# Four sparse graph layers on one core: own rows fetched before the variance's power, two PSUM buffers for the plain sums, nine places for own rows

## The chip, the cores and the metric

The kernel runs on one core of a Trainium2 chip. Its time is the device time of one execution in microseconds (us); the figure compared is the median over runs.

## The reference

Four graph layers follow each other on `x` (2708 × 512, float32) with one adjacency matrix `adj` (2708 × 2708), of which about 0.15% is not zero, besides the diagonal. Each layer is followed by a residual sum and a layer norm. The change acts on layer 1, and on buffers of layers 0 and 3.

```python
def _L1_gnn_ref(x, adj_a, adj_b, W_sa, a_sa, W_gcnb, b_gcnb, Wa, ba, Wb, bb):   # adj_a is adj_b here
    type_sum_a = adj_a @ x
    attn_a = sigmoid(concat([type_sum_a, x], 1) @ Wa.T + ba)      # attn_b: same with Wb, bb
    h = x @ W_sa
    scores = (h @ a_sa[0, :Hd])[:, None] + (h @ a_sa[0, Hd:])[None, :]
    e = where(adj_a != 0, exp(-leaky_relu(scores, 0.01)), 0.0)
    attn = e / (sum(e, 1, keepdims=True) + 1e-05)
    x_a = attn @ h
    x_b = adj_b @ (x @ W_gcnb) + b_gcnb
    return sigmoid(attn_a * x_a + attn_b * x_b)

x = layernorm(x + L0(x, adj, ...))     # L0: (x - (adj @ x) * (diag + 1)) @ W + b
x = layernorm(x + L1(x, adj, adj, ...))
x = layernorm(x + L2(x, adj))
x = layernorm(x + L3(x, adj, ...))
```

## The kernel before

The work is cut into 24 blocks of 113 rows of the graph. Layer 0 finds the non-zero entries of each block's rows (up to 512 in a block) and keeps them as a list; from then on a layer does not read `adj` any more. It fetches the rows that a block's list names, in four chunks of 128 (`gather`, four indirect DMAs issued by POOL, line 600), spreads the list into a small matrix of 128 × 113 per chunk, and lets PE multiply the two. The order of all instructions is written out by hand, engine by engine in program order; the tile framework adds the waits.

Layer 0 also writes, window by window of 128 rows, a table in DRAM (`table[0]`) with the two products `x @ W_sa` and `x @ W_gcnb` side by side and a few columns more, 1029 floats a row (`W1`). Layer 1 runs over the blocks in one loop (line 1629). Pass i, in program order:

- `gather1(i + 2)`: the fetch of the rows for block i + 2 (POOL), into one of three buffers `gath`.
- `sums1(i)`, line 1427: the plain sums of block i on PE, in a PSUM tile `l1s` of two banks. Its pool `ps_1s` has one buffer.
- `both1(i - 1)`, lines 1472 to 1487 (VectorE, called DVE; then a tanh on ScalarE, called ACT): takes the scored sums of block i − 1 out of PSUM, together with the block's own row of the table (`own1[i - 1]`). That is the last use of that own row.
- `values1`: spreads a list into a matrix, on ACT.
- `scored_sums1(i)`, line 1437: the sums weighted with `e`, on PE, in a PSUM tile `l1e` with one buffer (`ps_1e`).
- `scores1(i + 1)`, line 1410 on: the scores of the next block on DVE. It reads the fetched rows of block i + 1.
- `stats1(i - 1)`, lines 1492 to 1510: mean and variance on DVE. In every even pass the reciprocal root of two blocks' variances is computed as a power on POOL (line 1509).
- `gather_own1(i - 1 + NO)`, line 1382: one indirect DMA by POOL, which fetches a later block's own rows into the place that `both1(i - 1)` has freed. `NO` is 6, the number of places.
- `gates1(i)`, `gated1(i)`, lines 1447 to 1466: take the plain sums out of PSUM (DVE and ACT); line 1457 (`l1b`) reads the own row and is the last reader of the plain sums.
- `mask1(i + 1)`, `scale1`, `norm1(i - 2)`: the mask of the next block's scores, a factor from the power, and the finished rows of block i − 2, stored to `table[1]` by SP.

Each engine works through its own part of this list in order. The first six own rows are loaded by SP at the end of layer 0 (`load_own1`, two DMAs each). The six places lie in memory that layer 0 used for other things:

```python
    NO = 6

    def own_place(i):
        return (*shared, w0_own)[i % NO // 2][:, i % 2 * W1 :][:, :W1]
```

The buffers `xi` (two, the block's `x` rows), `uT` (two, a window turned for PE; also in layer 3) and `uw` (three, a window's inputs turned) of layer 0 come from a pool.

Of the kernel before, what the change touches and what calls it, by code (L numbers as in the profile page):

```python
# [8 lines left out]
FP = mybir.dt.float32  # L9
# [3 lines left out]
P = 128  # L13
# [434 lines left out]
def sparse_stack(  # L448
# [30 lines left out]
    N, D = x.shape  # L479
# [3 lines left out]
    NB = (N + R - 1) // R  # L483
    DB = D // P
# [79 lines left out]
    def move_rows(r, dst, src):  # L564

        c = r // 16 * 16
        for a, b in ((0, c), (c, r)):
            if a < b:
                nc.sync.dma_start(out=dst(a, b), in_=src(a, b))

    def turned(u, r, name):

        tr = ps_tr.tile([P, DB, P], FP, tag="tr", name=f"tr_{name}")
        for f in range(DB):
            nc.tensor.transpose(tr[:, f, :r], u[:r, f * P : (f + 1) * P], ident[:r, :r])
        uT = work.tile([P, DB, P], FP, tag="uT", name=f"uT_{name}")
        nc.scalar.copy(uT[:, :, :r], tr[:, :, :r])  # L577
        return uT

# [46 lines left out]

    w0_own = big.tile([P, 2 * W1], FP, name="w0_sb")
    w0_sb = w0_own[:, : DB * D].rearrange("p (b d) -> p b d", d=D)
    NO = 6

    def own_place(i):
        return (*shared, w0_own)[i % NO // 2][:, i % 2 * W1 :][:, :W1]

    def load_own1(i):
        r = rows(i)
        own1[i] = own_place(i)
        move_rows(
            r, lambda a, b: own1[i][a:b, 1 : 2 * D + 1],
            lambda a, b: table[0][i * R + a : i * R + b, 1 : 2 * D + 1],
        )  # L640
# [7 lines left out]
    with ExitStack() as phase:  # L648
# [40 lines left out]

        def load_own(i):  # L690
            r = rows(i)
            xi = work.tile([P, D], FP, tag="xi", name=f"xi{i}")
            move_rows(r, lambda a, b: xi[a:b, :], lambda a, b: x[i * R + a : i * R + b, :])
            return xi

# [122 lines left out]
        def turn_w(k):  # L818
            ps = ps_tr.tile([P, DB, P], FP, tag="tr", name=f"w_sa_t{k}")
            for f in range(DB):  # L820
                nc.tensor.transpose(ps[:, f, :], w_sa_sb[:, f, k * P : (k + 1) * P], ident)
            wT = work.tile([P, DB, P], FP, tag="uT", name=f"w_saT{k}")
            nc.scalar.copy(wT, ps)
            w_saT[k] = wT

# [225 lines left out]
        def store0(w):  # L1051
            r = wrows(w)
            st, o = st0.pop(w)
            nc.scalar.copy(st[:r, D + 1 : 2 * D + 1], o[:r, :])
            move_rows(
                r, lambda a, b: table[0][w * P + a : w * P + b, :], lambda a, b: st[a:b, :]
            )
# [3 lines left out]
        def turn_u(i):  # L1061

            u, r = u0.pop(i), rows(i)
            tr = ps_tr.tile([P, DB, P], FP, tag="tr", name=f"tr_l0_{i}")
            for f in range(DB):
                nc.tensor.transpose(tr[:, f, :r], u[:r, f * P : (f + 1) * P], ident[:r, :r])
            a = i * R
            while a < i * R + r:
                w = a // P
                b = min(i * R + r, (w + 1) * P)  # L1070
                if w not in window_uT:
                    window_uT[w] = work.tile(
                        [P, DB, P], FP, tag="uw", name=f"uw{w}", bufs=3
                    )
                nc.scalar.copy(
                    window_uT[w][:, :, a - w * P : b - w * P], tr[:, :, a - i * R : b - i * R]
                )
                a = b
# [130 lines left out]
        for k in range(NB + 2):  # L1209
            m = k + 2  # L1210
            w, wx, rest = window_at.get(k), window_at.get(k - 1), window_at.get(k - 1)
            bare = 2 < k < NB and w is None
            after = 2 < k < NB and wx is None
            parts = 4
            if any(t not in window_at for t in (k + 1, k + 2, k + 3)) and 2 < k < NB - 4:
                parts = 5
            if bare:
                parts, rest = 2, None
            if after:
                parts, rest = 3, window_at[k - 2]  # L1220
            if wx is not None and k <= NB:
                turn_x(wx)
            if m < NB:
                ranges(m)
                mark(m)
                fetch(m)
            if w is not None:
                project0(w)
            if k == 1:
                times_a(2)  # L1230
                times_a(3)
            if k == 0:
                times_a(0)
                turn_w(2)
            if unstored:
                store0(unstored.pop())
            if k + 3 < NB:
                negatives(k + 3)
            search(1)
            if m < NB:  # L1240
                pick(m)
                own[m] = load_own(m)
                values0(m)
            if k == 1:
                score_rows()
            if w is not None:
                bias0(w)
            search(1)
            if w is not None:
                residual0(w)  # L1250
            if window_at.get(k + 1, 0) > 1:
                load_window(window_at[k + 1])
            search(parts - 2)
            if wx is not None and not bare:
                next0(wx)
            if w is not None:
                norm0(w)
            if k + 1 < NB:
                sums0(k + 1)
                inputs0(k + 1)  # L1260
            if k == 1:
                score_columns()
            if k + 2 == NB:
                worst = check_lists()
                for i in range(4):
                    load_own1(i)
            if k == 0:
                times_a(1)
                turn_w(3)
            if bare:  # L1270
                starts(m + 1)
                next0(wx)
            elif rest is not None:
                rest0(rest, lambda: turn_x(w) if k == NB else starts(m + 1) if m + 1 < NB else None)
                unstored.append(rest)
            elif m + 1 < NB:
                starts(m + 1)
            if k + 1 < NB:
                turn_u(k + 1)
            if k == NB:  # L1280
                tell(worst)
                for i in range(4, NO):
                    load_own1(i)
        keep_busy(4)
        store0(KB - 1)


    gpool = ctx.enter_context(tc.tile_pool(name="gpool", bufs=1))
# [65 lines left out]
    nc.vector.memset(root, -0.5)  # L1354
    edge_s, edge_e, sum_s, sum_e, vb1, gate1, v1, mv2, unscaled = ({} for _ in range(9))
    phase = ctx.enter_context(ExitStack())
    ps_1s = phase.enter_context(tc.tile_pool(name="ps_1s", bufs=1, space=bass.MemoryType.PSUM))
    ps_1e = phase.enter_context(tc.tile_pool(name="ps_1e", bufs=1, space=bass.MemoryType.PSUM))
    ps_sp = phase.enter_context(tc.tile_pool(name="ps_sp", bufs=2, space=bass.MemoryType.PSUM))

# [19 lines left out]
    def gather_own1(i):  # L1380
        own1[i] = own_place(i)
        nc.gpsimd.indirect_dma_start(
            out=own1[i],
            out_offset=None,
            in_=table[0][:, :],
            in_offset=bass.IndirectOffsetOnAxis(ap=own_at[:, i : i + 1], axis=0),
            bounds_check=last,
            oob_is_err=False,
        )
# [17 lines left out]
    def scores1(i):  # L1407

        e = spool.tile([P, EC, R], FP, tag="e", name=f"e{i}")
        nc.vector.tensor_tensor(  # L1410
            e, gath[i % NGB][:, :, SR : SR + 1].to_broadcast([P, EC, R]),
            over_chunks(s_left[:, i, :]), ALU.add,
        )
        nc.vector.scalar_tensor_tensor(e, e, 0.01, e, op0=ALU.mult, op1=ALU.max)
        nc.scalar.activation(e, e, AF.Exp, scale=-1.0)
        edge_e[i] = e
# [212 lines left out]
    for i in range(NB):  # L1629
        if i + 2 < NB:  # L1630
            gather1(i + 2)
        sums1(i)
        if i > 0:
            both1(i - 1)
        if i + 2 < NB:
            values1(i + 2, (0, 1))
        scored_sums1(i)
        if i + 1 == NB:
            turn_norm(0)
            turn_norm(1)  # L1640
        if i + 1 < NB:
            scores1(i + 1)
        if 0 < i < NB - 1:
            stats1(i - 1)
        if 0 < i and i - 1 + NO < NB:
            gather_own1(i - 1 + NO)
        gates1(i)
        if i + 2 < NB:
            values1(i + 2, (2, 3))
        gated1(i)  # L1650
        if i + 1 < NB:
            mask1(i + 1)
        else:
            stats1(i - 1)
        scale1()
        if i > 1:
            norm1(i - 2)
        if i + 1 == NB:
            norm1(i - 1)
        if i + 1 == NB:  # L1660
            nc.sync.dma_start(out=b3_bc[0:1, :], in_=b3[None, :])
            nc.sync.dma_start(out=w3_sb, in_=w3T.rearrange("(b p) o -> p b o", p=P))
        if i < KB:
            source_sum(i)
        if i == KB:
            source_sums_out()
            row_norms(slice(0, KB))
# [243 lines left out]
```

## Time and profile before

| | us |
|---|---|
| median of 3 runs (lowest, highest) | 967.66 (964.5, 969.7) |
| the profiled execution: its own time | 978.13 |
| the profiled execution: span from first to last instruction | 976.3 |
| layer 0, until the first fetch of layer 1 | 413.9 |
| layer 1's passes, first plain sum to last scored sum | 421.9 to 614.7 |
| first sum of layer 2; of layer 3 | 630.0; 782.6 |

| engine | busy us | share of the span |
|---|---|---|
| PE matmul | 890.9 | 91% |
| DVE | 685.3 | 70% |
| ACT | 525.3 | 54% |
| POOL | 466.5 | 48% |

The profile comes from one execution. Times in it are microseconds from the first instruction. A row names the start, the duration, the engine, the line of the kernel, the operation, and what is written from what is read; a number in brackets behind it is how long the engine stood idle just before, and what ended that. "issue" there means that the profile shows nothing that the engine waited for. PE is the matmul engine, PEld its weight loads, SP issues plain DMAs. The shares above are averages over stages with different limits.

### The profile page before, as it was taken

To read this page: it belongs to the slowest core of one execution; us is meant where nothing else is said; L and a number is where in the kernel's file an instruction comes from. 1 tells how busy PE (TensorE), PEld (TensorE's weight loads), DVE (VectorE), ACT (ScalarE), POOL (GpSimd) and SP (SyncE) were. 2 spreads that over 40 slices of the span, in tenths; PEclk is the share of its full clock that TensorE was granted. 3 is DMA by queue.
4 is the path that set the end of the run, shared out by engine and by line. 5 is a ranking of instruction groups with operands and counts; after the bars stand their busy time and mean duration, and the time that the engine had idled before them with its cause. 6 is when DMAs were issued, how large, how long until landed. Compare 5 with 4: busy or idle time off the path is not lost.

```text
span 976.3 us, 11098 instructions
## 1 busy us (share of the span) xinstructions
PE 890.9 (91%) x2957; PEld 495.5 (51%) x2957; DVE 685.3 (70%) x1811; ACT 525.3 (54%) x1221; POOL 466.5 (48%) x521
## 2 busy tenths in 40 slices
PE   6789999999999999998989899787878799999993
PEld 2445556555555655466767677323333334444441
DVE  7787899878898843168988888756766526555553
ACT  5686667867668743357777776333445313222221
POOL 3223232423133320067777664476767278776730
PEclk7789999999999999979999999897999889999997
DMA  9987786978887534388898985466767266555531
GB/s 243 314 205 198 213 238 188 280 215 225 221 232 223 152 116 147 105 294 300 311 337 310 333 310 179 130 195 184 220 193 220 88 176 180 166 166 170 150 106 32
DMA packets 133758, 201.72 MB, mean 207 GB/s; under 512 B 82700, under 2 KB 82746, under 8 KB 133689
## 3 DMA queue, kind: packets, MB, share of 16 engines
q0 software_dynamic: 39456, 120.08, 39.7%
q1 hardware_dynamic: 94233, 80.86, 28.9%
q8 instruction: 25, 0.41, 0.2%
q14 instruction: 44, 0.36, 0.1%
HBM read 183.00 MB, written 27.80 MB: 216 GB/s over the span
## 4 chain that ended last, share of the span: by engine, by line
PE 62%; DVE 12%; DMA 8%; issue 6%; ACT 3%; POOL 3%; SPq 2%; another core or an unknown queue 2%; DVEq 0%; POOLq 0%; ACTq 0%
PE o_l L584 15%; PE l3a L613 9%; PE hb L584 7%; PE h L584 7%; PE l0a L613 6%; PE l2a L613 6%; DMA gath<-table,source 5%; POOL gath L600 2%; PE l1s L1427 2%; PE fetched L915 2%; PE unread L1571 2%; SPq L677 1%; PE l1e L1437 1%; DMA gath<-in_x_dram 1%
## 5 line engine op out<-in xcount | busy, mean ns | idle before, releaser
L600 POOL DMA_INDIRECT gath<-table,source x288 | 305.4, 1061 | 117.8 <-issue 86.1
L600 POOL DMA_INDIRECT gath<-in_x_dram,source x96 | 97.2, 1013 | 224.9 <-issue 192.1
L1427 PE MATMUL l1s<-gath,s 128*113 128x256 f32 (+3 forms) x384 | 93.9, 399 | 16.0 <-DVE l1b L1457 13.2
L613 PE MATMUL l2a<-gath,s_left 128*113 128x512 f32 (+1 forms) x192 | 95.2, 635 | 4.8 <-DMA gath<-table,source 3.6
L613 PE MATMUL l3a<-gath,s 128*113 128x512 f32 (+1 forms) x192 | 89.5, 610 | 2.8 <-DMA gath<-table,source 2.8
L1427 PEld LDWEIGHTS l1s<-gath,s 128*113 128x113 f32 (+1 forms) x384 | 68.8, 184 | 41.7 <-DVE l1b L1457 18.9
L613 PE MATMUL l0a<-gath,s 128*113 128x512 f32 (+1 forms) x192 | 87.3, 597 | 0.0
L584 PE MATMUL o_l<-shared,uT_l 128*113 128x512 f32 (+1 forms) x192 | 86.4, 592 | 0.7 <-ACT uT_l L577 0.7
L1437 PE MATMUL l1e<-gath,e 128*113 128x257 f32 (+3 forms) x384 | 87.0, 379 | 0.0
L584 PE MATMUL hb<-w_gc_sb,uT_x 128*128 128x512 f32 (+1 forms) x176 | 83.3, 601 | 0.0
L584 PE MATMUL o_l<-w_sb,uw 128*128 128x512 f32 (+1 forms) x176 | 82.5, 613 | 0.2
L584 PE MATMUL h<-w_sa_sb,uT_x 128*128 128x259 f32 (+1 forms) x352 | 80.8, 382 | 0.0
L1437 PEld LDWEIGHTS l1e<-gath,e 128*113 128x113 f32 (+1 forms) x384 | 68.1, 177 | 15.2
L584 PEld LDWEIGHTS h<-w_sa_sb,uT_x 128*128 128x128 f32 (+1 forms) x352 | 64.8, 185 | 19.8 <-issue 6.1
L1571 PE MATMUL unread<-bg_bc,ident 128*128 128x512 f32 x80 | 43.0, 652 | 23.9 <-remote 19.6
L1830 ACT ACTIVATE y<-l3v,mv_l 113x512 f32<-113x512 f32 (+1 forms) x24 | 19.5, 813 | 82.7 <-DVE mv_l L1826 72.6
L613 PEld LDWEIGHTS l2a<-gath,s_left 128*113 128x113 f32 (+1 forms) x192 | 34.1, 191 | 56.7 <-issue 40.0
L584 PEld LDWEIGHTS o_l<-shared,uT_l 128*113 128x113 f32 (+1 forms) x192 | 34.0, 178 | 48.7 <-issue 47.5
L1804 DVE SCALAR_TENSOR_TENSOR l3v<-o_l,d_inv,b_bc 113x512 f32<-113x512 f32 (+1 forms) x25 | 18.1, 729 | 51.5 <-PE o_l L584 50.7
L613 PEld LDWEIGHTS l3a<-gath,s 128*113 128x113 f32 (+1 forms) x192 | 33.0, 182 | 41.7 <-issue 39.7
L613 PEld LDWEIGHTS l0a<-gath,s 128*113 128x113 f32 (+1 forms) x192 | 33.8, 179 | 40.0 <-issue 36.3
L862 DVE FIND_INDEX8 where_all<-rec_all,shared 128x8 uint32<-128x678 f32 (+1 forms) x64 | 51.2, 800 | 0.0
(250 smaller groups left out, 1593.6 us busy)
## 6 DMA issues: line engine op xcount, KB each, us to landing
shared<-in_adj_dram SPq DMA_DIRECT2D x14, 1186.5 KB
table<-st SPq DMA_DIRECT2D x21, 514.5 KB
gath<-in_adj_dram SPq DMA_DIRECT2D x7, 1186.5 KB
gath<-in_x_dram SPq DMA_DIRECT2D x21, 256.0 KB
xi<-in_x_dram SPq DMA_DIRECT2D x23, 224.0 KB
table<-xr SPq DMA_DIRECT2D x23, 224.0 KB
table<-y SPq DMA_DIRECT2D x23, 224.0 KB
out_dram<-y SPq DMA_DIRECT2D x23, 224.0 KB
```

Of the source, the lines that this page charges most:

```text
L584: nc.tensor.matmul(o, lhsT=uT[:, f, :r], rhs=w[:, f, :], start=(f == 0), stop=(f == DB - 1))
L600: nc.gpsimd.indirect_dma_start(out=g[:, c, :n], out_offset=None, in_=src[:, :], in_offset=bass.IndirectOffsetOnAxis(ap=source[:, i, c : c ...
L613: nc.tensor.matmul(agg[:r, :], lhsT=s[:, c, :r], rhs=g[:, c, off : off + D], start=(c == 0), stop=(c == EC - 1),)
L677: nc.sync.dma_start(out=a[:TAIL, NF, :r], in_=adjT[NF * P :, at])
L862: nc.vector.max_index(out=where_all[:, i, g * 8 : (g + 1) * 8], in_max=top, in_values=seg)
L915: nc.tensor.matmul(t["fetched"][:, c, : 3 * NS], lhsT=t["q"][:, c * P : (c + 1) * P], rhs=rec_all[:, i].rearrange("p k s -> p (k s)"), sta ...
L1427: nc.tensor.matmul(sum_s[i][:r, k, : at.stop - at.start], lhsT=s[:, c, :r], rhs=g[:, c, at], start=(c == 0), stop=(c == EC - 1),)
L1437: nc.tensor.matmul(sum_e[i][:r, k, k : k + at.stop - at.start], lhsT=e[:, c, :r], rhs=g[:, c, at], start=(c == 0), stop=(c == EC - 1),)
L1571: nc.tensor.matmul(o[:, :cols], lhsT=ident, rhs=bg_bc[:, :cols], start=True, stop=True)
L1804: nc.vector.scalar_tensor_tensor(v[:r, at], o[:r, at], d_inv[:r, i : i + 1], b3_bc[:r, at], op0=ALU.mult, op1=ALU.add,)
L1830: nc.scalar.activation(y[:r, :], v[:r, :], AF.Identity, bias=mv[:r, 3:4], scale=mv[:r, 2:3])
```

## The change

Three things are edited, and the memory for one of them is found by a fourth.

- In each pass of layer 1 the fetch of an own row is issued before `stats1`, thus on POOL before the power, where it stood behind it.
- The pool of the plain sums gets two buffers in place of one: four PSUM banks where it had two.
- `NO` goes from 6 to 9. Rows 4 to 6 are loaded where 4 and 5 were, and rows 7 and 8 after the last store of layer 0; the fetches in the loop then begin with row 9.
- The places 6 to 8 lie in two new tiles, `uw_own` and `xi_own`. These hold, as slices, what were pool tiles before: `uw` (three), `xi` (two) and `uT` (two), used in the same turn as before.

```diff
+    def next_uT():
+        uT_ring.append(uT_ring.pop(0))
+        return uT_ring[-1]
...
-        uT = work.tile([P, DB, P], FP, tag="uT", name=f"uT_{name}")
+        uT = next_uT()
...
-    NO = 6
+
+    uw_own = big.tile([P, 3 * D], FP, name="uw_own")
+    uw_ring = [uw_own[:, k * D : (k + 1) * D].rearrange("p (b i) -> p b i", i=P) for k in range(3)]
+    xi_own = big.tile([P, max(4 * D, 2 * W1)], FP, name="xi_own")
+    xi_ring = [xi_own[:, k * D : (k + 1) * D] for k in range(2)]
+    uT_ring = [
+        xi_own[:, k * D : (k + 1) * D].rearrange("p (b i) -> p b i", i=P) for k in range(2, 4)
+    ]
+    NO = 9
 
     def own_place(i):
-        return (*shared, w0_own)[i % NO // 2][:, i % 2 * W1 :][:, :W1]
+        k = i % NO
+        t = (*shared, w0_own, uw_own, xi_own)[(k + (k >= 7)) // 2]
+        return t[:, (k + (k >= 7)) % 2 * W1 :][:, :W1]
...
-            xi = work.tile([P, D], FP, tag="xi", name=f"xi{i}")
+            xi = xi_ring[i % 2]
...
-            wT = work.tile([P, DB, P], FP, tag="uT", name=f"w_saT{k}")
+            wT = next_uT()
...
-                    window_uT[w] = work.tile(
-                        [P, DB, P], FP, tag="uw", name=f"uw{w}", bufs=3
-                    )
+                    window_uT[w] = uw_ring[w % 3]
...
             if k == NB:
                 tell(worst)
-                for i in range(4, NO):
+                for i in range(4, 7):
                     load_own1(i)
         keep_busy(4)
         store0(KB - 1)
+        for i in range(7, NO):
+            load_own1(i)
...
-    ps_1s = phase.enter_context(tc.tile_pool(name="ps_1s", bufs=1, space=bass.MemoryType.PSUM))
+    ps_1s = phase.enter_context(tc.tile_pool(name="ps_1s", bufs=2, space=bass.MemoryType.PSUM))
...
         if i + 1 < NB:
             scores1(i + 1)
+        if 0 < i and i - 1 + NO < NB:
+            gather_own1(i - 1 + NO)
         if 0 < i < NB - 1:
             stats1(i - 1)
-        if 0 < i and i - 1 + NO < NB:
-            gather_own1(i - 1 + NO)
         gates1(i)
```

## The prediction

> **What bounds the kernel now.** The change acts in layer 1, where a loop runs 24 passes, 0 to 23, one for each block of 113 rows. I read three views, in this order: busy time by stretch, to see who is nearly full; VectorE's (DVE's) rows in order of time, to see where that engine stops; the chain of waits, to see why. The first is the stretch from the start of pass 1 to that of pass 22; its columns are PE, PEld, DVE, ACT and POOL busy, PE clock, DMA share, GB/s.
>
> ```profile
> 433.87:601.28 167.41, 152.54 (x674) 118.58 (x673) 147.06 (x378) 123.49 (x315) 116.97 (x111) 0.99 0.89 312
> ```
>
> These are 21 passes in 167.41 us, 7.97 each. PE looks fullest, but its own work is 3.45 us of plain sums and 3.46 of scored sums per block, 6.9 in all (blocks 20 to 21, 585.40 to 592.34, where it never stops: 6.94). What does not show as busy on DVE is mostly short gaps between dependent operations. I therefore take its pace from starts. Each pass begins on DVE with the `rec` row of `both1`:
>
> ```profile
> 488.75 0.15 DVE L1472 SCALAR_TENSOR_TENSOR rec<-l1e,ediag 113x1 f32<-113x1 f32 x1
> ...
> 491.61 0.63 DVE L1410 TENSOR_TENSOR e<-gath,s_left 128x452 f32<-128x452 f32 x1 [0.77 <-issue]
> ...
> 497.40 0.15 DVE L1472 SCALAR_TENSOR_TENSOR rec<-l1e,ediag 113x1 f32<-113x1 f32 x1
> ...
> 504.86 0.15 DVE L1472 SCALAR_TENSOR_TENSOR rec<-l1e,ediag 113x1 f32<-113x1 f32 x1
> ```
>
> An odd pass (497.40 to 504.86) takes 7.46 us, and every odd pass takes 7.45 to 7.47: DVE goes straight through. An even pass, which also prepares the variance and its power, takes 7.80 where DVE does not wait (441.34 to 449.14) and more where the `e` row of `scores1` waits for gathered rows. Passes 2 to 20 last 7.80, 9.07, 8.16, 8.65, 8.33, 8.84, 8.51, 8.46, 9.28, 8.29. With 7.80 as floor the excess is 0, 1.27, 0.36, 0.85, 0.53, 1.04, 0.71, 0.66, 1.48, 0.49: **7.4 us**. Check: 11 × 7.46 + 10 × 7.80 = 160.06, and 167.41 − 160.06 = 7.35. So DVE sets the pace, and 7.4 us is all that better timing can bring in this stretch.
>
> Why the rows come late is in the chain:
>
> ```profile
> 510.60 0.46 POOL mv_l L1509
> ...
> 512.87 0.26 POOL gath L600
> ...
> 516.96 6.08 DMA gath<-table,source
> ```
>
> and on POOL's rows between these (shown here one pair of passes earlier):
>
> ```profile
> 492.01 1.10 POOL L600 DMA_INDIRECT gath<-table,source  x1 [0.30 <-issue]
> 494.74 0.71 POOL L1509 TENSOR_TENSOR mv_l<-mv_l,root 113x2 f32<-113x2 f32 x1 [1.63 <-DVE gate L1447]
> 495.63 1.07 POOL L1382 DMA_INDIRECT shared<-table,own_at  x1 [0.19 <-issue]
> 497.00 0.99 POOL L600 DMA_INDIRECT gath<-table,source  x1 [0.30 <-issue]
> ```
>
> POOL waits 1.63 us for the power's input, does the power (L1509), then issues the own rows (L1382), and only then the next block's four gathers. The last of those lands 6.08 us after its issue, just too late for the `e` two passes on. Power to power this loop takes 526.90 − 510.60 = 16.30 us; DVE alone needs 7.46 + 7.80 = 15.26. The POOL loop is longer, and closes through DVE's wait.
>
> **What the Trainium skill says.** "Perfetto Trace Analysis", Optimization Strategy: a gap that repeats on the engine that should be saturated can mean too few buffers. Here a gap repeats on PE, which is not that engine:
>
> ```profile
> PE l1s L1427 <- DVE l1b L1457: 13.2, 13, 2.0
> POOL mv_l L1509 <- DVE gate L1447: 23.9, 11, 9.2
> ```
>
> So I give the buffer no time of its own. "PSUM — Partial Sum Buffer", PSUM bank collisions raise a hardware error: two engines must not touch a bank at once, two readers included. The trace agrees: L1457 (DVE) waits 0.32 us in nearly every block for the copy L1451 (ACT) of the same sums. A second buffer leaves this pair in one bank, so 0.32 stays inside the floors. "DMA: Bandwidth & Descriptors", Issuing engines are not separate DMA queues: transfers from SP and POOL share 16 engines and only issue time is saved. In the trace the share is about 1.0 from 485 to 496 us, at a mean of 379 GB/s.
>
> **The change, part by part.**
>
> *Own rows ahead of the power (even passes).* Both instructions stay. The fetch needs its place free, that is `both1`'s L1478 done: 489.24 + 0.73 = 489.97, while POOL is idle from 493.11. So it goes out at 493.4, inside the 1.63 us wait, and ends at 494.5, before the power's input at 494.7. The gathers behind the power come 497.00 − 495.64 = 1.36 us earlier. The POOL loop falls from 16.30 to 14.94, under DVE's 15.26. Hence nearly all of the 7.4 goes. Should POOL be late, the power queues behind the fetch and up to 1.4 us passes to `scale1` on DVE; that reads it at 497.03, 1.58 after the power's end, so this is covered. What can be late next: with 0.32 us of slack, a landing slower than 6.08 (I see 5.9 to 6.5) brings back up to 0.1 to 0.4 in some passes. I take 0.6 us left over ten passes; bounds 0 and 5.4, the latter if landings follow the DMA's backlog and not the issue (below).
>
> *Two PSUM buffers.* L1427 no longer waits for L1457 (13.2 us). Scored sums keep one buffer, so PE next waits at L1437 for `both1`'s L1478. Per odd pass: L1478 ends 1.19 us after `rec`, scored sums then run 3.5, plain sums 3.4, so PE is back after some 8.2 us, 0.7 into the next pass, and waits about 0.5. It gains nothing, but scored sums end about 0.6 earlier and free the gathered rows; POOL waited 5.3 us in four places for that, in early passes and at 584.38. A loss is excluded: PE's order is the same, it only starts earlier, and the three pools take 4 + 2 + 2 banks, which the layer has to itself. I take 0; the other bound is a gain of 0.5, pass 20's excess, already in the 7.4.
>
> *Nine places.* POOL loses three fetches, those of passes 16 to 18: 3 × 1.36 = 4.1 us of POOL time, off the path, since DVE holds it; it makes pass 18 (the 1.48) safer. SP gains three loads of two issues each, about 0.3 us an issue. Row block 6: 0.6 us on SP at 404, before the store of window 20 and the moves at 407.19, which wait for ACT anyway. Its 113 × 4096 B = 0.46 MB take 1.2 us at 379 GB/s; the DMA share falls to 0.24 at 408 to 410, so it fits there. If not, `ediag` at 410.13 comes up to 1.2 later, and ACT takes its result only at 412.07, after a table load; ediag's two last DVE operations end at 410.76, so 1.3 us cover it. Rows 7 and 8: four issues, 1.2 to 1.5 us from 411.47, where SP stands waiting until 413.08 for the last store; behind them is only `bg_bc`, which PE needs at 419.92. Their 0.93 MB need 2.4 us. The DMA share is 0.10, 0.01, 0.00 from 412 to 415 and gathered data flow from 415, so they fit, just. Block 1's `e` (429.12) waits 2.01 for gathers already, so what overlaps is paid in full. I take +0.3; bounds 0 and 2.4.
>
> *Slices in place of pool tiles* (`uw`, `xi`, `uT`): same number of slots, same order of use, no instruction added. I take 0; below.
>
> Sum: −7.4 + 0.6 + 0.3 = −6.5 us. The profiled execution took 978.13 (span 976.3) and would take 971.6. It stands 10.5 above the median of 967.66; nothing says that the waits differ there, so I carry the 6.5 over: **961.2**. About 0.5% (4.8 us) is what a measurement of this kernel can tell from no change.
>
> **Rivals.**
>
> *Landings follow the backlog (0.20).* For it: the share averages 0.89 and reads 1.0 for 11 us of each pair of passes. By share the stretch has 0.89 × 167.4 = 149 us of DMA, against 160.06 of DVE. Against it: the share falls to 0.58 and 0.68 at 496 to 498, right behind POOL's stop, so an earlier issue finds idle engines. If it holds, only the excess of passes 18 and 20 (2.0 us), where fetches fall away, is won: 965.7.
>
> *The start pays (0.10).* The two late loads meet the first gathers and cost their whole 2.4 us, with the rest as forecast: about 963.6.
>
> *Slower: slices wait like whole tiles (0.08).* If an access to `xi_own` waited for all others to that tile, turning a window (`uT`, ACT) would wait for the `x` rows in flight to the same tile. Layer 0 is a PE chain with turn, `h` and `hb` in it, 22 windows; one landing per window, some 1.6 us (moves issued until 408.5 land at 410.1), is 35 us: 996. From 0.5 us a window it eats the gain and ends slower. Against it: `gath` and `shared` already hold slices with different uses in layer 0, without such waits. That the buffer does not do what it says (PE's wait moves to L1437) is in my forecast, at no price.
>
> **How the numbers follow.** My case has 0.62 and lies between 957 (all 7.4, and some 3 for the spread of the runs, 964.5 to 969.7) and 962.8. The next two end within 0.5%, 0.30 together; the fourth slower, 0.08. Range: 957 to 968, the top being the backlog's 965.7 and the runs' spread; it leaves out the fourth and the tails.
>
> **What would show it.** Right: in layer 1 L1382's counterpart stands before the power in every even pass; `e` waits for gathers fall from some 6.5 us in passes 2 to 20 to under 1.5; even passes last 7.8 to 7.9, odd ones still 7.46; PE's waits on `l1b` are gone, with waits on `l1a` in their place. Wrong: even passes over 8.2 with POOL ahead (backlog); block 1's `e` later than 429.6 counted from the first gather at 413.93 (start); layer 0 longer than now, when the first gather starts at 413.93 (slices); odd passes off 7.46, either way, would overturn the bound itself.

## The result and the profile after

The kernel with the change takes **958.98 us** (median of 11 runs, 954.93 to 963.22); the kernel before, run on the same chip in turn with it, takes 967.53 (11 runs, 963.59 to 970.87). The ratio is **0.9921, 95% interval 0.9898 to 0.9944**: a gain of 7.6 us, between 5.4 and 9.9. (The ratio is worked out over all runs and not from the two medians, which lie 8.6 us apart.) The profiled execution took 958.69, with a span of 956.9. The kernel is faster, by 0.8%; the forecast was 961.2.

The first view is again the busy time from the start of pass 1 to that of pass 22, of the kernel after. Columns: the stretch and its length, PE, PEld, DVE, ACT and POOL busy, PE clock, DMA share, GB/s.

```profile
433.71:593.84 160.13, 150.72 (x674) 117.45 (x673) 146.35 (x380) 123.17 (x315) 113.08 (x107) 1.00 0.90 316
```

The length is what counts: 160.13 us where it was 167.41. DVE's floor, worked out ahead as 11 × 7.46 + 10 × 7.80, was 160.06. So the stretch stands 0.07 us above the floor. Below, I call "excess" what the even passes 2 to 20 last beyond 7.80 each: it was 7.4 us, now it is −0.03.

VectorE's rows, after, an even pass (502.14 to 509.94) and an odd one (509.94 to 517.39):

```profile
502.14 0.15 DVE L1486 SCALAR_TENSOR_TENSOR rec<-l1e,ediag 113x1 f32<-113x1 f32 x1
...
504.13 0.62 DVE L1424 TENSOR_TENSOR e<-gath,s_left 128x452 f32<-128x452 f32 x1
...
509.94 0.15 DVE L1486 SCALAR_TENSOR_TENSOR rec<-l1e,ediag 113x1 f32<-113x1 f32 x1
...
517.39 0.15 DVE L1486 SCALAR_TENSOR_TENSOR rec<-l1e,ediag 113x1 f32<-113x1 f32 x1
```

The `e` row has no bracket any more: DVE comes to it without having waited, here and in all passes from 1 on. The even pass lasts 7.80, the odd one 7.45. GpSimd's rows between them, after:

```profile
503.80 1.28 POOL L604 DMA_INDIRECT gath<-table,source  x1 [0.30 <-issue]
505.38 1.51 POOL L1396 DMA_INDIRECT shared<-table,own_at  x1 [0.30 <-issue]
507.35 0.72 POOL L1523 TENSOR_TENSOR mv_l<-mv_l,root 113x2 f32<-113x2 f32 x1 [0.46 <-DVE gate L1461]
508.25 1.06 POOL L604 DMA_INDIRECT gath<-table,source  x1 [0.19 <-issue]
```

The own rows' fetch (L1396) now fills the time in which POOL waited for the power's input; what is left of that wait is 0.46 us, and the next gather follows the end of the power 0.19 later. From the start of the power to that of this gather it is 0.90 us, where it was 2.28 (means of nine pairs of passes). And the waits from 410 to 610 us, after (who, for whom: us in all, times, longest):

```profile
PE l1e L1451 <- DVE l1a L1492: 10.4, 23, 0.7
...
DVE l1b L1471 <- ACT row_cnt L1465: 8.5, 24, 0.8
...
DVE e L1424 <- DMA gath<-table,source: 4.0, 2, 2.5
```

PE's wait for `l1b` (13.2 us before) is gone; in its place PE waits at L1451 for `l1a`, 10.4 us. DVE's wait for gathers is left in two places only, both ahead of pass 1.

**Where the gain is.** Layer 1 as a whole, from its first gather to layer 2's first sum, fell from 216.1 us (413.9 to 630.0) to 208.0 (414.26 to 622.3): 8.1, of which 7.3 lie in the stretch above. The two profiled spans differ by 19.4, but most of the rest is layer 2, which the change doesn't touch: it took 152.6 us in the first profile of before, 142.0 after, and 143.7 in a second profile of before (`e5_before_again`).

### The profile page after: what moved, and what is told of

Same layout as the page of the kernel before. It is cut to its first block, busy times and chain, and to the rows that moved or that the text cites. A ratio compares the mean times of both kernels' runs of the same rounds, so it can differ in the third digit from the quotient of the medians.

```text
span 956.9 us, 11163 instructions
## 1 busy us (share of the span) xinstructions
PE 884.8 (92%) x2957; PEld 489.4 (51%) x2957; DVE 685.3 (72%) x1811; ACT 526.3 (55%) x1221; POOL 465.5 (49%) x518
## 4 chain that ended last, share of the span: by engine, by line
PE 58%; DMA 14%; DVE 14%; issue 5%; ACT 4%; SPq 3%; POOL 2%; POOLq 0%; DVEq 0%; ACTq 0%
PE o_l L588 15%; DMA gath<-table,source 11%; PE l3a L617 8%; PE hb L588 7%; PE h L588 7%; PE l0a L617 6%; PE l2a L617 2%; PE fetched L929 2%; POOL gath L604 2%; PE unread L1585 2%; DVE l1b L1471 1%; SPq L691 1%; DMA gath<-in_x_dram 1%; DVE l1b L1475 1%; DVE l1a L1492 1%
## 5 line engine op out<-in xcount | busy, mean ns | idle before, releaser
L617 PE MATMUL l2a<-gath,s_left 128*113 128x512 f32 (+1 forms) x192 | 97.2, 624 | 17.6 <-DMA gath<-table,source 17.4
L1451 PE MATMUL l1e<-gath,e 128*113 128x257 f32 (+3 forms) x384 | 88.4, 383 | 10.4 <-DVE l1a L1492 10.4
L1441 PE MATMUL l1s<-gath,s 128*113 128x256 f32 (+3 forms) x384 | 89.8, 387 | 0.0
L588 PE MATMUL o_l<-shared,xi_own 128*113 128x512 f32 (+1 forms) x192 | 86.5, 593 | 0.8 <-ACT xi_own L581 0.7
L588 PE MATMUL hb<-w_gc_sb,xi_own 128*128 128x512 f32 (+1 forms) x176 | 83.3, 601 | 0.0
L1451 PEld LDWEIGHTS l1e<-gath,e 128*113 128x113 f32 (+1 forms) x384 | 66.2, 177 | 32.7 <-PE l1s L1441 19.4
L588 PE MATMUL o_l<-w_sb,uw_own 128*128 128x512 f32 (+1 forms) x176 | 82.7, 614 | 0.2
L588 PE MATMUL h<-w_sa_sb,xi_own 128*128 128x259 f32 (+1 forms) x352 | 80.8, 382 | 0.0
L588 PEld LDWEIGHTS h<-w_sa_sb,xi_own 128*128 128x128 f32 (+1 forms) x352 | 64.8, 185 | 19.8 <-issue 6.1
L617 PEld LDWEIGHTS l2a<-gath,s_left 128*113 128x113 f32 (+1 forms) x192 | 30.4, 181 | 73.9 <-DMA gath<-table,source 53.9
L588 PEld LDWEIGHTS o_l<-shared,xi_own 128*113 128x113 f32 (+1 forms) x192 | 33.9, 177 | 49.2 <-issue 47.1
L1308 DVE TENSOR_SCALAR s<-niota_r,nrow,edges 128x113 f32<-128x113 f32 x192 | 51.5, 344 | 0.0
```

What stands on the lines that cost most here:

```text
L588: nc.tensor.matmul(o, lhsT=uT[:, f, :r], rhs=w[:, f, :], start=(f == 0), stop=(f == DB - 1))
L617: nc.tensor.matmul(agg[:r, :], lhsT=s[:, c, :r], rhs=g[:, c, off : off + D], start=(c == 0), stop=(c == EC - 1),)
L1308: nc.vector.tensor_scalar(s[:, c, :], niota_r, nrow[:, i, c : c + 1], edges[:, i, c, 1:2], op0=ALU.is_equal, op1=ALU.mult,)
L1441: nc.tensor.matmul(sum_s[i][:r, k, : at.stop - at.start], lhsT=s[:, c, :r], rhs=g[:, c, at], start=(c == 0), stop=(c == EC - 1),)
L1451: nc.tensor.matmul(sum_e[i][:r, k, k : k + at.stop - at.start], lhsT=e[:, c, :r], rhs=g[:, c, at], start=(c == 0), stop=(c == EC - 1),)
```

## The experiments

Three questions: which part brought the gain, what is late next, and whether POOL's instruction or its place was the trouble. Each ratio is against the kernel before on the same chip; the chips differ from group to group. "Stretch" is pass 1 to pass 22 in the profiled execution, one for each row. That of "PSUM alone" was the quickest of its 22 runs; those of "before, counts copied earlier" and of "the same on another chip" were the slowest of theirs.

| kernel | stretch | excess | median us | before beside it | ratio (95%) |
|---|---|---|---|---|---|
| before, first profile | 167.41 | 7.4 | 967.53 | | |
| before, second profile | 167.96 | 7.9 | | | |
| after | 160.13 | 0.0 | 958.98 | 967.53 | 0.9921 (0.9898 to 0.9944) |
| swap alone | 160.54 | 0.4 | 959.18 | 964.87 | 0.9950 (0.9936 to 0.9964) |
| PSUM alone | 165.84 | 5.6 | 963.68 | 964.87 | 0.9984 (0.9971 to 0.9998) |
| after without the swap | 164.69 | 4.0 | 962.83 | 964.87 | 0.9979 (0.9964 to 0.9995) |
| after with one PSUM buffer | 160.85 | 0.8 | 957.56 | 964.87 | 0.9932 (0.9906 to 0.9958) |
| after with six places | 160.47 | 0.4 | 956.51 | 964.59 | 0.9921 (0.9892 to 0.9950) |
| after, counts copied earlier | 158.11 | | **951.21** | 964.59 | 0.9875 (0.9841 to 0.9908) |
| before, counts copied earlier | 167.74 | | 963.16 | 964.59 | 0.9994 (0.9976 to 1.0012) |
| before, own rows by SP | 172.07 | 11.9 | 981.51 | 978.26 | 1.0044 (1.0023 to 1.0064) |
| the same on another chip | 172.30 | 12.0 | 968.15 | 966.29 | 1.0022 (1.0007 to 1.0038) |
| after, own rows by SP | 172.30 | 11.6 | 982.32 | 978.26 | 1.0048 (1.0022 to 1.0074) |
| counts earlier and SP | 169.85 | | 980.64 | 978.26 | 1.0028 (1.0010 to 1.0045) |

### Which part it was

**The swap alone**, on the kernel before:

```diff
-        if 0 < i < NB - 1:
-            stats1(i - 1)
         if 0 < i and i - 1 + NO < NB:
             gather_own1(i - 1 + NO)
+        if 0 < i < NB - 1:
+            stats1(i - 1)
```

> The kernel before with one edit: the own rows' fetch is issued ahead of the power; one PSUM buffer for the plain sums and six places stay. Measured by the stretch from the rec row of pass 1 to that of pass 22 (167.41 us before, 160.13 after, floor of VectorE 160.06). Theory A (the fetch between the power and the gathers makes the gathered rows late): 160.1 to 161.5 us, even passes 7.8 to 7.9, median about 960 to 961.5. Theory B (the second PSUM buffer brings the gain): 166.5 to 167.5, median about 967. Theory C (fewer fetches in the loop and preloaded rows bring it): above 165, median about 966.

Measured: stretch 160.54, excess 0.36, so 6.9 of the 7.3 us come with the two statements changing places and nothing else. One `e` row in passes 2 to 20 still waits for gathers (0.34). By the run times the swap brings 4.8 us (3.5 to 6.2 by the interval of the ratio), somewhat less than the stretch says.

**The second PSUM buffer alone**, on the kernel before:

```diff
-    ps_1s = phase.enter_context(tc.tile_pool(name="ps_1s", bufs=1, space=bass.MemoryType.PSUM))
+    ps_1s = phase.enter_context(tc.tile_pool(name="ps_1s", bufs=2, space=bass.MemoryType.PSUM))
```

> The kernel before with one edit: two PSUM buffers for the plain sums. Stretch of passes 1 to 22. Theory A: PE's wait moves from l1b to l1a and the stretch stays at 166.5 to 167.4, of which pass 20 alone may lose its 0.5; median about 967. Theory B: 160 to 162, median about 960. Theory C: 167.4.

Its waits, 410 to 610 us:

```profile
PE l1e L1437 <- DVE l1a L1478: 14.1, 20, 1.9
```

PE's wait has moved on to L1437 and is as long as the one that it replaced. Stretch 165.84: 1.6 us less than the first profile of before, 2.1 less than the second. By the ratio it is 1.5 us (0.2 to 2.8). DVE's `e` rows still wait in most even passes.

**The change without the swap** (the two statements back in the old order, as in the first diff reversed):

> The changed kernel with the fetch put back behind the power; two PSUM buffers and nine places stay. Theory A: even passes up to 14 keep their excess over 7.80 (4.8 us in all), pass 16 and later, which have no fetch, lose theirs (2.6 us): stretch 164.5 to 165.5, median about 965. Theory B: 160 to 161, median about 960. Theory C: 160 to 162.

Measured: 164.69. Passes 18 and 20 have no excess; those from 4 to 16 keep one. Nine places save the three fetches of passes 16 to 18. In the old order the fetch of pass 16 stands ahead of the gathers that `e` of pass 18 needs, and that of pass 18 ahead of those for pass 20: take the fetch away, and the excess goes. That pass 16 itself would lose its excess was expected and wrong, by one pair of passes: its gathers stand behind the fetch of pass 14, which stays (0.98 us of excess). Against the PSUM buffer alone the places bring 1.15 us.

**The change with one PSUM buffer** (`bufs=1` again):

> The changed kernel with one PSUM buffer for the plain sums; the swap and nine places stay. Theory A: stretch 160.1 to 160.7 as in the changed kernel (160.13), PE waits for l1b as before, some 8 us in all; median about 959 to 960. Theory B: 166 to 167.4, median about 966. Theory C: 160 to 161.

Measured: 160.85, all of the excess in one pass (pass 4, 8.65).

**The change with six places** (all slices and the three late loads undone; swap and PSUM buffer stay):

```diff
-    NO = 9
+    NO = 6
...
-                for i in range(4, 7):
+                for i in range(4, NO):
...
-        for i in range(7, NO):
-            load_own1(i)
```

> The changed kernel with six places and the old buffers; the swap and two PSUM buffers stay. Theory A: stretch 160.1 to 160.6 (the swap alone gave 160.54, all three 160.13), median about 957 to 960. Theory C (places matter by themselves): 162 or more. If the late loads cost anything at the start, this kernel is the quicker one from the first gather to pass 1 (19.45 us in the changed kernel), by up to 2.4 us.

Measured: 160.47 and a median of 956.51. With the swap in, the places bring 0.3 us of the stretch and the PSUM buffer 0.1 to 0.7, each the size of one late landing in one pass. That is about what the stretch of one kernel varies by (0.6, just below), so an effect of either beside the swap is not shown. By the stretch the gain is the swap's. The run times say the same less sharply: 4.8 us (3.5 to 6.2) for the swap and 7.6 (5.4 to 9.9) for the whole, on different chips, leave room for a us or two from the others.

**The kernel before, profiled once more:**

> The kernel before, unchanged, profiled once more. The first profile of it spent 152.6 us from layer 2's first sum to layer 3's, the five profiles of other kernels so far 141 to 143. Theory A (the change ends with layer 1; that profile was a long one, 978 us against a median near 966): layer 2 takes 141 to 143 us here too, the stretch of passes 1 to 22 takes 165.5 to 167.5, and the time is 963 to 970. Theory D (the change also helps layer 2, by where its PSUM banks fall): layer 2 takes 150 us or more here.

```profile
429.81:597.77 167.96, 151.21 (x674) 117.45 (x673) 147.16 (x380) 123.64 (x315) 116.27 (x111) 1.00 0.89 311
```

The stretch repeats within 0.6 us (two profiles), while the two spans (976.3 and 963.1) lie 13 apart. That is why the parts are told apart by stretch and not by span.

### What is late next

In the floor of 160.06 each block holds the 0.32 us in which DVE's `l1b` waits for ACT's copy `row_cnt` of the same plain sums. The copy can stand earlier in ACT's program order, right after the last block's tanh:

```diff
+    def counts1(i):
+        r = rows(i)
+        nc.scalar.copy(row_cnt[:r, i, :], sum_s[i][:r, 1, H + 3 : H + 5])
...
     def gates1(i):
...
-        nc.scalar.copy(row_cnt[:r, i, :], sum_s[i][:r, 1, H + 3 : H + 5])
...
             both1(i - 1)
+        counts1(i)
         if i + 2 < NB:
             values1(i + 2, (0, 1))
```

**On the kernel after:**

> The changed kernel with one move: ACT's copy of the row counts out of the plain sums is issued right behind both1 and no longer between the gates and l1b, so that l1b does not wait 0.32 us for it in each pass. VectorE's floor falls to 7.14 and 7.48, 14.6 a pair. Theory A (VectorE bound, POOL's loop next at 14.8 to 14.9): stretch 154.5 to 157 us, POOL's wait at the power near zero while own rows are fetched, median about 954. If something else than VectorE set the pace of the changed kernel: stretch stays near 160.

**On the kernel before:**

> The kernel before with the same move of the row counts' copy. VectorE's floor falls by 0.32 us a pass, 6.7 us over the stretch. Theory A (in the kernel before POOL's loop through the own rows' fetch sets the pace, VectorE only waits for it): what VectorE saves comes back as longer waits of e for gathered rows; stretch 164.5 to 167.4, median about 964 to 966. Rival (VectorE itself sets the pace before, and the waits for rows are chance): stretch about 160.7, median about 958.

On the kernel before it gives nothing (stretch 167.74, ratio 0.9994). Most odd passes fall to about 7.06 us, and what DVE saves it then waits: its `e` rows wait longer, up to 2.27. DVE was not what set the pace there. On the kernel after, it takes another 2.0 us off the stretch and gives the fastest kernel of all, **951.21 us**, 13.4 under the kernel before and 5.3 under the six-place version on the same chip (six runs each). The stretch accounts for 2.4 of these 5.3; the rest is not accounted for. The stretch was to be 154.5 to 157; it is 158.11. POOL's rows show why, here with the copy moved on the kernel after:

```profile
460.11 0.99 POOL L1396 DMA_INDIRECT shared<-table,own_at  x1 [0.30 <-issue]
461.12 0.74 POOL L1526 TENSOR_TENSOR mv_l<-mv_l,root 113x2 f32<-113x2 f32 x1
462.03 1.06 POOL L604 DMA_INDIRECT gath<-table,source  x1 [0.18 <-issue]
...
476.13 0.73 POOL L1526 TENSOR_TENSOR mv_l<-mv_l,root 113x2 f32<-113x2 f32 x1
```

The power has no bracket: its input was there, and POOL does not stop for anything but the 0.3 us between two fetches. From power to power it needs 15.01 us for eight gathers, two own fetches and the power, and DVE, which could do a pair of passes in 7.05 + 7.45 = 14.50, waits for it. After the change DVE's 15.26 and POOL's 15.0 stand almost level; past that, POOL's list is the bound where own rows are fetched (15.0 to 15.6 us a pair up to the power at 537.07). In the two pairs after 552.05 none is fetched, POOL waits 2.4 us at each power, and a pair still takes 14.9 us. There the loop through the landing is the longest: from the power at 566.93 it is 0.91 to the first gather, 4.48 to the fourth, 6.30 until `e` has its rows and 3.22 to the next power, 14.91 in all.

### Own rows from another queue

The own rows of a block lie side by side in the table, so SP can load them, as it does for the first six. If POOL's load is the trouble, the fetch should go there:

```diff
         if 0 < i and i - 1 + NO < NB:
-            gather_own1(i - 1 + NO)
+            load_own1(i - 1 + NO)
```

**On the kernel before:**

> The kernel before, with the own rows in the loop loaded by SP (two plain DMAs, as at the end of layer 0) in place of POOL's indirect one; order, PSUM buffers and six places stay. POOL then has nothing between the power and the gathers, and 1.3 us less to do per pass. Theory A (what cost the time was POOL's issue of the fetch in its loop): stretch of passes 1 to 22 at 160.1 to 161 us although the same bytes move, median about 958 to 960. Rival (the DMA engines are the limit, and the swap helped by spacing the transfers): 164 us or more.

**On the kernel after:**

> The changed kernel with the own rows in the loop loaded by SP. Theory A (VectorE is the bound of the changed kernel, POOL has some slack): nothing to gain, stretch 160.0 to 160.5, median as the changed kernel's, about 957 to 959. If POOL still held it back: below 159.

**With the copy moved as well:**

> The changed kernel with ACT's copy of the row counts moved behind both1 and the own rows in the loop loaded by SP. With the copy moved alone the stretch came to 158.11, POOL going without a stop at 15.0 us a pair against VectorE's 14.5. Theory A: with POOL relieved by 2.6 us a pair VectorE's floor is reached, 11 x 7.06 + 10 x 7.45 = 152.2, with some waits for rows left 152.5 to 155 us; median about 946 to 949. Rival (the DMA engines are next, share 0.94 in the first part of the loop): 156.5 to 158.5, median about 951.

All three went against the expectation: stretches of 172.07, 172.30 and 169.85, each slower than the kernel before on the same chip. POOL has less to do (93.4 us busy in the stretch where it had 116.3) and is idle more. On that chip the kernel before took 978, not 965, so the chip itself could have been the cause. The first of the three was run again on another:

> The kernel before with the own rows in the loop loaded by SP, once more. Its first run came to a stretch of 172.07 us, 4 us slower than the kernel before beside it, on a chip on which that kernel took 978 us and not 965. If the kernel makes it (SP's loads start as soon as both1 has freed the place, while the gathers that the next e needs are in flight, and take transfer time from them): stretch 170 to 173 us on any chip, slower than the kernel before by 3 to 5 us. If that chip made it (slower transfers) and theory A holds elsewhere: stretch 160 to 162 on a chip where the kernel before takes about 965, and about 958 us.

There the kernel before takes 966.29, and the stretch is 172.30 again: it is the kernel, not the chip (the kernel before has no profile on these two chips; elsewhere its stretch was 167.41 and 167.96). By the ratio it is 2.1 us slower than before (0.7 to 3.7), less than the 3 to 5 expected. Two views show what happens. The first is POOL's rows and, in the second box, the one DVE row that counts, of this last run:

```profile
480.37 0.71 POOL L1509 TENSOR_TENSOR mv_l<-mv_l,root 113x2 f32<-113x2 f32 x1 [4.79 <-DVE gate L1447]
481.26 1.06 POOL L600 DMA_INDIRECT gath<-table,source  x1 [0.19 <-issue]
...
485.24 1.26 POOL L600 DMA_INDIRECT gath<-table,source  x1 [0.30 <-PE l1s L1427]
...
496.64 0.71 POOL L1509 TENSOR_TENSOR mv_l<-mv_l,root 113x2 f32<-113x2 f32 x1 [3.91 <-DVE gate L1447]
```

```profile
493.51 0.63 DVE L1410 TENSOR_TENSOR e<-gath,s_left 128x452 f32<-128x452 f32 x1 [0.97 <-DMA gath<-table,source]
```

Here the loop can be added up. From the power to the first gather 0.89; to the fourth one's issue 3.98; until `e` has its rows 8.27; from `e` to the next power 3.13: 16.27 us from power to power. In the kernel before the same sum was 0.89 + 1.37 (own fetch) + 4.16 + 6.21 + 3.23 = 15.86 (494.74 to 510.60), with these two rows for the fourth gather and `e`:

```profile
501.16 0.99 POOL L600 DMA_INDIRECT gath<-table,source  x1 [0.30 <-issue]
```

```profile
507.37 0.63 DVE L1410 TENSOR_TENSOR e<-gath,s_left 128x452 f32<-128x452 f32 x1 [0.44 <-issue]
```

The fetch is gone from it, and the landing has grown by more. Over nine pairs the means are 16.56 and 16.09. The second view is of the DMA issues from 440 to 584 us, with the last number as the median us from issue to landing; first the kernel before, in its second profile, then the SP version:

```profile
gath<-table,source POOLq DMA_INDIRECT x74, 6.7
```

```profile
gath<-table,source POOLq DMA_INDIRECT x70, 8.1
```

A gather lands 1.4 us later at the median. For the last gather of a block where `e` waits for it, it is 8.7 us against 6.6 (means of 9 and 8 cases). With 8.7 in place of 6.6, the kernel after loses its slack too: 0.89 + 4.0 + 8.7 + 3.1 = 16.7, over DVE's 15.26; its run shows 16.53 (481.28 to 497.81).

So the result is what the rival named ahead of the first of these runs foretold: 164 us or more, if the DMA engines are the limit and the swap helped by spacing the transfers. For the swap itself its second half does not hold: with the swap alone a gather lands as fast as before (median 6.6 us, 6.7 before), and what falls is the time from the power to the next gather.

Why the gathers land later beside SP's loads is argued, not shown. SP moves no more bytes: 181.83 MB are read from HBM in the executions with its loads, 183.00 in those of the kernel before. The Trainium skill, "DMA: Bandwidth & Descriptors", SWDGE vs HWDGE vs iDMA, says that DMAs issued by POOL and by SP feed different queues inside each DMA engine, which takes turns between them. If so, 0.46 MB of own rows from SP go between the gathers in flight, instead of behind them as they would in POOL's own order; in the pair above SP issues them at 484.50, just ahead of the fourth gather at 485.24. A version that issues the SP load at another moment, or in smaller pieces, would test it; it was not run.

## Why the prediction held, point by point

- **DVE sets the pace, and 7.4 us is what there is to win.** Right: stretch 160.13 against a floor of 160.06. I called DVE the bound of the kernel before; more exactly, it was its floor. The loop through POOL's program order, the landing and DVE set the pace, as the early copy on the kernel before shows: it lowers DVE's floor and the stretch stays. That 7.4 us is all that better timing can bring holds for this order of ACT's list only; with the copy moved the floor itself falls, and the stretch to 158.11. Odd passes were to stay at 7.46: they do, but for two late ones of 7.52 and 7.53.
- **The fetch goes into POOL's wait, and the gathers come 1.36 earlier.** Right (1.38, from 2.28 to 0.90 behind the power's start): L1396 stands before L1523 in each even pass that has one, and the wait left over is 0.34 to 0.46 us there, where 0.2 followed from its times (fetch done at 494.5, input there at 494.7). The total of POOL's waits at the power hardly moved (23.9 to 22.0), because in the late passes without a fetch it waits 2.3 to 3.9; a total over a layer would have hidden the effect.
- **0.6 us left over ten passes.** Too careful: 0.07. In the three other kernels with the swap and the copy in its old place it is 0.4 to 0.8, nearly all in one pass each, so part of the 0.07 may be luck.
- **The second buffer at 0.** Not contradicted with the swap in (0.1 to 0.7 by the pairs of runs, about what the stretch varies by), too low without it: 1.6 to 2.1 alone by the stretch, 1.5 (0.2 to 2.8) by the run times. I put its upper bound at 0.5. That PE would then wait at L1437 about 0.5 per block is right (10.4 us in 23 places). Most of the 1.6 to 2.1 lies between the fourth gather and `e`: 6.35 us with two buffers, 6.49 and 6.53 in the two profiles of before, on the mean of nine pairs. Why those gathers land sooner the profiles don't settle: POOL's waits for scored sums are no shorter there in total. The Trainium skill, "Perfetto Trace Analysis", Optimization Strategy, says that a gap that repeats can mean a lack of buffers where it is on the engine that should be full; here the gap on PE repeats with either number of buffers (13.2 us with one, 14.1 with two).
- **Nine places at +0.3, bounds 0 and 2.4.** Right in size, not by its working. The moves to `xr` land later: `ediag` starts 4.5 to 5.0 us after SP begins to issue the last two of them in the six kernels with nine places, 2.6 to 3.2 in the eight executions without. Row 6's load, issued 3.2 us ahead of them in the changed kernel, is the likely cause; the same six kernels have the slices too, and no run parts the two. These 1.8 us exceed the 1.2 that I had from bytes at 379 GB/s, and the 1.3 of cover. They shift the first gather by 0.2 to 0.5 us only (6.9 to 7.2 after that issue, against 6.7, every time). The rows are:

```profile
407.06 1.28 SPq L569 DMA_DIRECT2D xr<-gath  x2
...
411.44 1.36 SPq L569 DMA_DIRECT2D xi_own<-table  x4
```

```profile
411.79 0.20 DVE L1322 TENSOR_TENSOR ediag<-xr 128x24 f32<-128x24 f32 x1 [8.54 <-DMA xr<-gath]
...
429.35 0.63 DVE L1424 TENSOR_TENSOR e<-gath,s_left 128x452 f32<-128x452 f32 x1 [2.46 <-DMA gath<-table,source]
```

  Rows 7 and 8 take 1.36 us of SP, as worked out, and cost nothing that shows: from the first gather to pass 1 it is 18.9 to 19.8 us with them and 18.7 to 19.9 without (own rows by SP in the loop left aside). The six-place version was to be quicker here by up to 2.4 if they cost anything; it takes 18.9 where the changed kernel takes 19.45, inside this spread.
- **Slices at 0.** Right: the first gather starts at 413.3 to 414.3 in the six kernels with slices, at 409.4 to 415.7 in the eight executions with pool tiles; a wait for each window would have been 35 us. The few us are those between executions (413.9 and 410.5 for the kernel before); a cost of a us or two would not show.
- **The rivals.** That landings follow the backlog is refuted: with the fetch ahead the gathers land as fast as before (median 6.6 after, 6.7 before) and the excess goes in all passes. That the start pays its 2.4 us is refuted by the time from the first gather to pass 1: 19.45 after, 19.94 and 19.32 before.
- **The carry-over.** The sum gave −6.5, and 6.5 was carried to the median. By the ratio 7.6 came (5.4 to 9.9), by the medians 8.6. Of the 1.1 between 6.5 and 7.6 the left-over, 0.5 too high, explains one half. The rest of layer 1 was 0.8 shorter outside the stretch, but the way to pass 1 alone varies by a us from one execution to the next, and the remainder is well inside the interval.

## What to carry to other kernels

When an engine runs its list in order and issues transfers as well as computing, look for an instruction on it that waits, and ask what stands behind it: an independent transfer put ahead of that instruction goes out in time that was lost anyway. Add up the loop (issue, landing, use, back to the next issue) and compare it with the floor of the engine that seems to bound. Here trimming that engine paid only once the loop was the shorter, and the next longest loop was close behind. Moving a transfer to another queue is a different change from moving it in its own: it takes issue time off one engine and can delay the transfers that it now runs beside.

## What the runs showed of the hardware

- An own row block of 0.46 MB loaded by SP beside POOL's gathers put their landing from 6.6 to 8.7 us in the cases that counted; a single such load ahead of layer 1 is the likely cause of a landing 1.8 us later of a few small moves. The Trainium skill, "DMA: Bandwidth & Descriptors", Issuing engines are not separate DMA queues, says that issuing from several engines saves only issue time; here it saved that (1.37 us of the loop in the pair shown), and the landing grew by 2.06.
- In layer 1 an indirect fetch of up to 128 rows occupies POOL for 1.0 to 1.5 us, with 0.3 between two. Eight gathers, two own fetches and the power, one right behind the other, took 15.01 us with the copy moved (461.12 to 476.13), and a pair of passes of the changed kernel 15.3.
- Two readers of one PSUM tile on two engines cost a wait of 0.32 us in nearly every block (8.5 us in 24 places). The Trainium skill, "PSUM — Partial Sum Buffer", PSUM bank collisions raise a hardware error, says that two engines must not touch one bank at once, so a wait is to be expected. With the small reader moved ahead in its engine's order the wait of `l1b` is gone (0.7 us is left, once, at another row), and the odd pass is 0.40 shorter.
